# Two transformer blocks on one core: context products in 64x64 tiles, a sixth buffer for MLP weights, constants in one allocation

## The chip, the cores and the metric

The kernel runs on one core of a Trainium2 chip. Time is device time in microseconds of that core, and a kernel's time is the median of its runs. Everything is in fp32. The engines are named as in the profile: PE (TensorE, with PEld for its weight loads), DVE (VectorE), ACT (ScalarE), POOL (GpSimd) and SP (SyncE, which here issues all DMAs, in order).

## What is computed

The input `x` has 32 sequences of 64 tokens with 512 features. Two blocks follow one another. The first is attention with 8 query heads and one shared key and value head of size 64, rotary positions, and then a gated MLP of width 2048; both normalisations are RMS with a scale that depends on the sequence. The second is attention with 16 heads of size 32 over 4 key and value heads that come out of a latent of 128, with a layer norm whose scale and shift depend on the sequence. Cut to what matters:

```python
# block 0
h = ada_rms(x, t, ln1_w, ln1_tw)
q, k, v = h @ Wq.T, h @ Wk.T, h @ Wv.T            # 8 heads of 64; one k, one v
q, k = rope(q), rope(k)
attn = softmax(q @ k.T / sqrt(64))                # within a sequence of 64
x = x + (attn @ v) @ Wo.T
h = ada_rms(x, t, ln2_w, ln2_tw)
x = x + (silu(h @ Wg.T) * (h @ Wu.T)) @ Wd.T      # 512 -> 2048 -> 512
# block 1
h = ada_layernorm(x, t)
q = h @ Wq.T; c = h @ Wkd.T; k = c @ Wku.T; v = c @ Wvu.T
x = x + attention(rope(q), rope(k), v) @ Wo.T
```

## The kernel before

The 2048 tokens are cut into 8 units of 256 tokens (4 sequences). A unit lives in SBUF as `x[128, 4, 256]`: features on partitions, in four chunks, tokens in the free dimension. For each unit there are three pieces of work: `attention0` (block 0's attention and the norm of the MLP), `mlp`, and `attention1`.

**MLP.** Each of the three weight matrices is multiplied by seven products of halves (Strassen's scheme) instead of eight. One "set" is a buffer `[128, 7, 256]` with the three quarters of weights that are used as they are, and four sums of them. For the first unit, a set is loaded as three quarters (384 KB, `set<-in_wmlp`) and a fourth one (128 KB, `a<-in_wmlp`), `combine` makes the four sums on DVE and POOL, and they are stored to DRAM (512 KB, `sums<-set`). From the second unit on the sums are loaded back (`set<-sums`). Three sets (gate, up, down) serve one of eight pairs of hidden tiles; 192 sets in all pass through `MW` = 5 buffers with the tag `mw`. `load_sets` issues the next load when `done_with` says that a set is used up. `first_products` and `last_products` make the products `gu`, `gated` the activations, `down` the second matmul.

**attention0** is a generator that yields (cost, latency) after each piece. Queries `q0` and the pair of keys and values `kv0` are projected with weights stationary and tokens moving. Values are turned by transposes `vt` and copied by ACT into `vblk0`, which holds, for each sequence, a block-diagonal matrix of 128 x 128: the values in the upper left for the even heads and in the lower right for the odd heads, zeros elsewhere. These zeros are written once, by POOL (`early`). Probabilities `p` are transposed in two halves `t` (`turned`: four transposes into a bank `pp`, and a copy by ACT to `pT`), and for each half two matmuls of K=128, M=128, N=256 make the context `cx`, which two ACT copies per half of 128 x 256 bring to `cT`. `output` then multiplies `cT` with `wo0` in two halves, `po`, and adds to `x`.

**Order.** The instructions of the first two attentions are recorded in the order of the string `FIRST` ("a" is unit 0, "b" unit 1, "m" the modulations), and on PE this order is binding. They run before there is any MLP work. After that the class `Order` mixes the MLP of unit u, `attention0` of unit u+1, and `attention1` of earlier units, always the one that is least advanced among those whose latency is over. A scheduler of the framework then sorts each engine's queue further, and inserts the waits. PSUM has 8 banks: two with the tag `at` for all attention work beside the MLP, two `gu`, four `acc` for the `down` sums.

**At the end** the last two units' `attention1` run without MLP, with buffers borrowed from elsewhere (`sixth`, `seventh`); the seventh takes the first `vblk0`, zeroed again, for its values.

Constants and weights that stay (`ident`, `spread`, `small`, `kblk0`, `vblk0`, `wqkv`, `wo0` and so on) are each a tile of their own, made by `fixed`.

Of the kernel before, what the change touches and what calls it, by code (L numbers as in the profile page):

```python
# [10 lines left out]
F32 = mybir.dt.float32  # L11
# [6 lines left out]
P = 128  # L18
B, S, D = 32, 64, 512
# [25 lines left out]
TURN = (0.15911865234375, 3.628432750701904e-05, 6.4192136051133275e-09, 1.4247115856860781e-12)  # L45
ROUND = 12582912.0
WARM = 11
FIRST = "aaaaaaa bb a mm aa b a b aa bbb a b aa a bb a mmmm a bbbb".replace(" ", "")
TWO_PI = float(np.nextafter(np.float32(2 * np.pi), np.float32(0)))


# [56 lines left out]
def two_blocks(ctx: ExitStack, tc: tile.TileContext, a: dict, out: bass.AP):  # L108
# [17 lines left out]
        homes["n"] += 1  # L126
        return bank(tags[homes["n"] % len(tags)], name)

    def fixed(tag, shape, dtype=F32):
        return const.tile(shape, dtype, tag=tag, name=tag)  # L130

    def work(tag, shape, name, bufs=2):
        return wk.tile(shape, F32, tag=tag, name=name, bufs=bufs)


    ident = fixed("ident", [P, P])
    make_identity(nc, ident)
    ones = fixed("ones", [P, P])
    nc.gpsimd.memset(ones, 1.0 / D)

    idle = bank("at", "idle")
    for _ in range(WARM):
        nc.tensor.matmul(idle[:, :P], ones, ones, start=True, stop=True)

    spread = fixed("spread", [P, US, P])
    nc.gpsimd.memset(spread, 0.0)
    for q in range(US):
        rows = slice(q * HALF0, (q + 1) * HALF0)
        for i in range(2):
            block = ident[rows, rows][:, i * HALF1 : (i + 1) * HALF1].unsqueeze(1).unsqueeze(1)  # L150
            to = spread[rows, q].rearrange("p (r a h f) -> p r a h f", r=2, a=2, h=2)[:, :, i]
            nc.gpsimd.tensor_copy(to, block.to_broadcast([HALF0, 2, 2, HALF1]))
    eps0 = fixed("eps0", [P, 1])
    nc.gpsimd.memset(eps0, EPS0)
    eps1 = fixed("eps1", [P, 1])
    nc.gpsimd.memset(eps1, EPS1)
    quarter = fixed("quarter", [P, 1])
    nc.gpsimd.memset(quarter, float(np.float32(np.pi / 2)))

    positions = []  # L160
# [4 lines left out]
        positions.append(t)  # L165

    load_positions(0)
    small = fixed("small", [P, C_ALL])
    nc.sync.dma_start(small, a["small"])
    condT = small[:, C_COND:C_VECS].rearrange("p (k b) -> p k b", b=B)  # L170
    vecs = small[:, C_VECS:C_CS1]
# [3 lines left out]
    sign_of = small[:, C_SIGN:C_ALL]  # L175


    kblk0 = [fixed(f"kblk0{i}", [P, US, S]) for i in range(2)]

    vblk0 = [fixed(f"vblk0{i}", [P, US, 2, S]) for i in range(2)]  # L180
    vblk1 = [fixed(f"vblk1{i}", [P, US, 2, 2 * HD1]) for i in range(2)]

    s0a = fixed("s0a", [P, KC, B])
    s0b = fixed("s0b", [P, KC, B])
    s1 = fixed("s1", [P, KC, B])
    t1 = fixed("t1", [P, KC, B])
    angle = fixed("angle", [P, 2, NU * S])


    wqkv = [fixed("wqkv0", [P, KC, 384]), fixed("wqkv1", [P, KC, 256])]  # L190
    wo0 = fixed("wo0", [P, KC, D])
    wq1 = fixed("wq1", [P, KC, D])
    wkd = fixed("wkd", [P, KC, LAT])
    wkv1 = fixed("wkv1", [P, 2, P])
    wo1 = fixed("wo1", [P, KC, D])

    x_units = {}

# [4 lines left out]
        nc.sync.dma_start(xt, a["x"][u])  # L203
        x_units[u] = xt

    MW = 5

# [98 lines left out]
    def angles(u0):  # L308

        cols = slice(u0 * S, (u0 + 2) * S)  # L310

        def some(tag, name, cols=512, bufs=2):
            return work(tag, [P, cols], f"{name}_{u0}", bufs)[:, : 2 * S]

        posi = positions.pop()
        posf, sign = some("u", "posf"), some("v", "sign")
        both = work("p0", [P, 2, 512], f"ang_lo_{u0}", 1)
        ang, lo = both[:, 0, : 2 * S], both[:, 1, : 2 * S]
        hi, prod = some("pT0", "hi", 512, 1), some("r0", "prod", UT, 1)
        acc, rnd = angle[:, 0, cols], angle[:, 1, cols]  # L320
        nc.vector.tensor_copy(posf, posi)
        nc.vector.tensor_scalar(sign, posf, 0.0, None, ALU.is_ge)
        nc.vector.tensor_scalar(sign, sign, 2.0, -1.0, ALU.mult, ALU.add)
        nc.vector.tensor_tensor(posf, posf, sign, ALU.mult)
        nc.vector.tensor_scalar(ang, posf, freq, None, ALU.mult)
        nc.vector.scalar_tensor_tensor(lo, ang, 4097.0, ang, ALU.mult, ALU.subtract)
        nc.vector.scalar_tensor_tensor(hi, ang, 4097.0, lo, ALU.mult, ALU.subtract)
        nc.vector.tensor_tensor(lo, ang, hi, ALU.subtract)

        def fraction(dst, src):  # L330
            nc.vector.tensor_scalar(rnd, src, ROUND, ROUND, ALU.add, ALU.subtract)
            nc.vector.tensor_tensor(dst, src, rnd, ALU.subtract)

        first = True
        for piece, turn in ((hi, 0), (hi, 1), (lo, 0), (hi, 2), (lo, 1)):
            nc.vector.tensor_scalar(prod, piece, TURN[turn], None, ALU.mult)
            if first:
                fraction(acc, prod)
                first = False
            else:  # L340
                fraction(prod, prod)
                nc.vector.tensor_tensor(acc, acc, prod, ALU.add)
        nc.vector.scalar_tensor_tensor(acc, lo, TURN[2], acc, ALU.mult, ALU.add)
        nc.vector.scalar_tensor_tensor(acc, ang, TURN[3], acc, ALU.mult, ALU.add)
        fraction(prod, acc)
        nc.vector.tensor_scalar(lo, prod, 0.25, None, ALU.add)
        fraction(hi, lo)
        nc.scalar.activation(acc, hi, AF.Sin, scale=TWO_PI)
        nc.scalar.activation(rnd, prod, AF.Sin, scale=TWO_PI)
        nc.vector.tensor_tensor(rnd, rnd, sign, ALU.mult)  # L350
        if u0 + 2 < NU:
            load_positions(u0 + 2)
# [75 lines left out]
    def all_chunks(row):  # L428
        return row.unsqueeze(1).to_broadcast([P, KC, UT])

    RING = {"h": 2, "p1": 2, "pT1": 2}

    def space(room, tag, columns, name):

# [6 lines left out]
    def tile4(room, tag, name):  # L441
        return space(room, tag, KC * UT, name).rearrange("p (c t) -> p c t", t=UT)
# [126 lines left out]
    def attention0(u, room, early=None, late=None):  # L569
# [71 lines left out]
        vt = abank(f"vt_{u}").rearrange("p (b d) -> p b d", d=P)  # L641
        for b in range(US):
            nc.tensor.transpose(vt[:, b, :HD0], vT[HD0:, b].rearrange("p r s -> p (r s)"), ident[HD0:, HD0:])
        for i in range(2):
            rows = slice(i * S, (i + 1) * S)
            nc.scalar.copy(vb[rows, :, i, :], vt[rows, :, :HD0])
        yield 0.3, 4.5


# [23 lines left out]
            yield 0.5 * len(ts), 5.0 * ts[0] if lean else 10.0  # L673

        cT = tile4(room, "h", f"cT0_{u}")
        for t in range(2):
            pT = turned(ps[t], f"0_{u}_{t}", space(room, "pT", 512, f"pT0_{u}_{t}")).rearrange("p (c t) -> p c t", c=KC)
            yield 0.5, 1.2
            cx = abank(f"cx0_{u}_{t}").rearrange("p (b c s) -> p b c s", b=2, c=KC)
            for b in range(2):  # L680
                nc.tensor.matmul(  # L681
                    cx[:, b],
                    vb[:, 2 * t + b].rearrange("p r d -> p (r d)"),
                    pT[:, :, b * S : (b + 1) * S],
                    start=True,
                    stop=True,
                )
            to = cT[:, :, t * P : (t + 1) * P].rearrange("p c (b s) -> p b c s", s=S)
            for b in range(2):
                nc.scalar.copy(to[:, b], cx[:, b])  # L690
            yield 0.9, 1.5 * t
        yield from output(u, cT, wo0, f"0_{u}")


# [293 lines left out]
                load_sets(MW)  # L988

    def early():  # L990
        for z in (*vblk0, *vblk1):
            nc.gpsimd.memset(z, 0.0)

    def second(u, room=None):
# [61 lines left out]
    def spare(tag, cols, name, bufs=2):  # L1056
        return work(tag, [P, cols], f"own_{name}", bufs)

    nc.gpsimd.memset(vblk0[0], 0.0)
    two = [spare("h2", 1024, f"h2{i}") for i in range(2)]  # L1060
    few = spare("cs", 512, "few", 1)
    extra = spare("x", 1024, "kb6", XB)
# [5 lines left out]
        "latT": [few[:, :UT]],  # L1068
        "kr": [few[:, UT:]],
        "kb": [extra[:, :512]],  # L1070
        "pT": [extra[:, 512:], spare("pT0", 512, "pT6", 1)] * 2,
    }
    big = [spare("mw", 1792, f"mw{j}", MW) for j in range(4)]
    seventh = {
        "ring": "-",
        "lean": True,
        "vb": vblk0[0],
        "h": [big[0][:, :1024], big[1][:, :1024], big[1][:, :1024]],
        "latT": [big[0][:, 1024:1280]],
        "kr": [big[0][:, 1280:1536]],  # L1080
# [89 lines left out]
```

## Time and profile before

| what | value |
|---|---|
| median of 3 runs | 1061.24 us (1060.54 to 1062.72) |
| the profiled execution's own time | 1059.08 us |
| its span | 1057.3 us |
| mean granted PE clock | 0.989 |
| `gu` matmuls, two groups | 288.3 and 215.3 us busy |
| `down` matmuls, two groups | 136.4 and 109.2 us busy |
| `po`, largest group | 108.4 us busy, 480 instructions of 380 ns |
| context of attention 0 (`cx`, line 681) | 18.3 us busy, 64 instructions |
| bytes moved by DMA | 198.53 MB, mean 188 GB/s |

A row of a group gives its busy time, the mean duration of one instruction, and the idle time of the engine just before. Durations of PE instructions overlap, since they are pipelined, so what a block of them costs is read from the start of its first to the start of the next block in the timeline. A matmul of the program is two instructions of the same shape in the trace.

### The profile page before, as it was taken

To read this page: it belongs to the slowest core of one execution; us is meant where nothing else is said; L and a number is where in the kernel's file an instruction comes from. 1 tells how busy PE (TensorE), PEld (TensorE's weight loads), DVE (VectorE), ACT (ScalarE), POOL (GpSimd) and SP (SyncE) were. 2 spreads that over 40 slices of the span, in tenths; PEclk is the share of its full clock that TensorE was granted. 3 is DMA by queue.
4 is the path that set the end of the run, shared out by engine and by line. 5 is a ranking of instruction groups with operands and counts; after the bars stand their busy time and mean duration, and the time that the engine had idled before them with its cause. 6 is when DMAs were issued, how large, how long until landed. Compare 5 with 4: busy or idle time off the path is not lost.

```text
span 1057.3 us, 21448 instructions
## 1 busy us (share of the span) xinstructions
PE 1013.2 (96%) x8538; PEld 944.1 (89%) x8538; DVE 548.6 (52%) x1377; ACT 324.5 (31%) x682; POOL 434.7 (41%) x520
## 2 busy tenths in 40 slices
PE   7889999999999989999999998999999999999887
PEld 6779999998999989999999997999999899999765
DVE  4866646543455485343653268532755335452363
ACT  4333112344124242132422323331423422241132
POOL 4424545344255434254342543324533335432541
PEclk8989999999999999999999999999999999999899
DMA  7916896354556465662646555455735557565001
GB/s 276 328 43 219 294 312 240 136 210 151 203 210 210 143 217 177 227 222 105 224 172 221 184 182 183 150 203 203 251 118 196 173 189 284 197 230 178 11 1 40
DMA packets 68274, 198.53 MB, mean 188 GB/s; under 512 B 7248, under 2 KB 15184, under 8 KB 67792
## 3 DMA queue, kind: packets, MB, share of 16 engines
q1 hardware_dynamic: 68176, 197.17, 53.6%
q8 instruction: 68, 1.11, 0.4%
q14 instruction: 30, 0.25, 0.1%
HBM read 180.37 MB, written 16.78 MB: 186 GB/s over the span
## 4 chain that ended last, share of the span: by engine, by line
PE 79%; DVE 10%; POOL 5%; issue 2%; DMA 2%; ACT 1%; SPq 0%; ACTq 0%; POOLq 0%; DVEq 0%
PE gu L875 32%; PE down L934 16%; PE po L514 10%; PE q L514 9%; PE pp L549 2%; PE lat L514 1%; PE cx L681 1%; PE cx L845 1%; PE sc L821 1%; PE kv L514 1%; DMA set<-in_wmlp 1%; PE sc L664 1%; DVE mx L534 1%; DVE sm L542 1%; DMA x<-in_x 1%
## 5 line engine op out<-in xcount | busy, mean ns | idle before, releaser
L875 PE MATMUL gu<-h,set 128*128 128x128 f32 x2048 | 288.3, 276 | 8.9 <-DVE c L894 5.2
L875 PEld LDWEIGHTS gu<-h,set 128*128 128x128 f32 x2048 | 259.4, 192 | 15.9 <-issue 10.7
L875 PE MATMUL gu<-hc,set 128*128 128x128 f32 x1536 | 215.3, 275 | 0.0
L875 PEld LDWEIGHTS gu<-hc,set 128*128 128x128 f32 x1536 | 193.6, 192 | 0.5
L913 POOL TENSOR_TENSOR act<-c,c 128x384 f32<-128x384 f32 x64 | 66.6, 1040 | 193.6 <-DVE c L901 117.5
L934 PE MATMUL down<-td,set 128*128 128x128 f32 x1024 | 136.4, 276 | 3.2 <-POOL td L916 3.2
L934 PEld LDWEIGHTS down<-td,set 128*128 128x128 f32 x1024 | 125.1, 192 | 4.5 <-POOL td L916 4.2
L887 ACT COPY e<-gu 128x128 f32<-128x128 f32 x128 | 33.7, 265 | 279.1 <-PE gu L875 268.8
L901 DVE TENSOR_TENSOR c<-gu,u 128x256 f32<-128x256 f32 x128 | 53.4, 419 | 118.1 <-PE gu L875 117.8
L514 PE MATMUL po<-cT,wo 128*128 128x256 f32 x480 | 108.4, 380 | 2.4 <-DVE sm L542 2.1
L934 PE MATMUL down<-act,set 128*128 128x128 f32 x768 | 109.2, 278 | 0.0
L889 DVE TENSOR_TENSOR u<-e,gu 128x128 f32<-128x128 f32 x128 | 36.1, 282 | 130.4 <-ACT e L887 129.8
L514 PEld LDWEIGHTS po<-cT,wo 128*128 128x128 f32 x480 | 89.3, 190 | 14.2 <-ACT cT L854 2.6
L934 PEld LDWEIGHTS down<-act,set 128*128 128x128 f32 x768 | 97.9, 192 | 4.2 <-issue 2.4
L544 POOL TENSOR_TENSOR p<-p,sm 128x512 f32<-128x512 f32 x40 | 41.3, 1052 | 116.5 <-DVE sm L543 110.6
L525 POOL TENSOR_TENSOR qT<-u_q,v_q 128x512 f32<-128x512 f32 x30 | 38.1, 1270 | 93.8 <-DVE v_q L524 93.8
L562 DVE TENSOR_TENSOR x<-x,po 128x512 f32<-128x512 f32 x32 | 22.0, 687 | 75.9 <-PE po L514 75.9
L970 ACT ACT_TABLE_LOAD x34 | 43.6, 1283 | 55.8 <-DVE c L901 55.4
L514 PE MATMUL q<-h,wqkv 128*128 128x256 f32 x256 | 58.4, 380 | 0.0
L514 PE MATMUL q<-h,wq 128*128 128x256 f32 x224 | 52.1, 385 | 1.6 <-POOL h L750 1.6
L514 PEld LDWEIGHTS q<-h,wqkv 128*128 128x128 f32 x256 | 47.7, 191 | 6.4 <-issue 0.4
L915 POOL TENSOR_TENSOR td<-act 128x256 f32<-128x256 f32 x64 | 47.6, 744 | 10.0 <-DVE act L912 3.8
(276 smaller groups left out, 1407.4 us busy)
## 6 DMA issues: line engine op xcount, KB each, us to landing
set<-sums SPq DMA_DIRECT2D x168, 512.0 KB, 5.8
set<-in_wmlp SPq DMA_DIRECT2D x192, 384.0 KB, 4.7
sums<-set SPq DMA_DIRECT2D x24, 512.0 KB, 4.7
x<-in_x SPq DMA_DIRECT2D x8, 512.0 KB, 5.7
out_x<-x SPq DMA_DIRECT2D x16, 256.0 KB, 2.1
mod<-in_mod SPq DMA_DIRECT2D x7, 512.0 KB, 6.2
a<-in_wmlp SPq DMA_DIRECT2D x24, 128.0 KB, 4.3
wo<-in_wo SPq DMA_DIRECT2D x2, 1024.0 KB, 8.4
```

What stands on the lines that cost most here:

```text
L514: nc.tensor.matmul(ps, w[:, k, cols], h[:, k, :], start=(k == 0), stop=(k == KC - 1))
L525: nc.gpsimd.tensor_tensor(dst, u, v, ALU.add)
L544: nc.gpsimd.tensor_tensor(p8, p8, sm.unsqueeze(2).to_broadcast(wide), ALU.mult)
L562: nc.vector.tensor_tensor(x[:, part], x[:, part], po, ALU.add)
L875: nc.tensor.matmul(ps, w[:, slot, k * P : (k + 1) * P], b[of][:, k], start=start and k == 0, stop=k == 1, skip_group_check=True)
L887: nc.scalar.copy(e, ps[:, 0])
L889: nc.vector.tensor_tensor(u2, e, ps[:, 1], ALU.add)
L901: nc.vector.tensor_tensor(c.rearrange("p (a b) t -> p a b t", b=2)[:, :, 1], ps[:, 2:4], u2.unsqueeze(1).to_broadcast([P, 2, HT]), ALU.add,)
L913: nc.gpsimd.tensor_tensor(act[:, 1:4], gate[:, 1:4], c[:, 1:4], ALU.mult)
L915: nc.gpsimd.tensor_tensor(td[:, 0:2], act[:, 1:3], act[:, 0:2], ALU.subtract)
L934: nc.tensor.matmul(sums_of[u][p][:, c], w[:, slot, c * P : (c + 1) * P], b[of], start=q % NP == 0 and i % 2 == 0 and c == 0, stop=q % NP = ...
L970: nc.scalar.activation(gate[2][:, 0], gate[0][:, 0], AF.Silu)
```

## The change

- **Context of attention 0.** `vblk0` is no longer block-diagonal but `[128, 4, 64]`: the values of a sequence twice, above one another, filled by one ACT copy of 128 x 256 in place of two of 64 x 256. For each half `t`, each sequence `b` and each half of the rows `r` there is one matmul with K=64, M=64, N=256, so eight in place of four. The tiles lie at the four corners of the array: rows by `r`, columns by `b`. Results go to two banks, one per `r`. Both halves of `p` are transposed first, and `cT` is filled at the end by four ACT copies of 64 partitions x 512.
- **Order.** `attention0` has one yield fewer, other costs and latencies, and `FIRST` has one "a" less. The "bbbb" at its end now reaches into unit 1's first half of `po`.
- **Sets.** `MW` is 6.
- **One buffer.** `fixed` cuts its tiles out of a single one of 14103 columns, `stays`.
- **Small.** The angle computation takes three buffers of its own (`ang0` to `ang2`) in place of `p0` and `pT0`; `pT0` has two buffers; the zeros of `vblk0` and their memsets go; at the end the seventh's values get a zeroed buffer with the tag `pT1`.

The projections of queries and of outputs (`query`, `project`, `output`) are not touched by the diff.

```diff
-FIRST = "aaaaaaa bb a mm aa b a b aa bbb a b aa a bb a mmmm a bbbb".replace(" ", "")
+STAY = 14103
+FIRST = "aaaaaaa bb a mm aa b a b a bbb a b aa a bb a mmmm a bbbb".replace(" ", "")
...
+    stays = {"all": const.tile([P, STAY], F32, tag="stays", name="stays"), "at": 0}
+
+    def fixed(shape):
+        n, i = int(np.prod(shape[1:])), stays["at"]
+        stays["at"] += n
+        t = stays["all"][:, i : i + n]
...
-    vblk0 = [fixed(f"vblk0{i}", [P, US, 2, S]) for i in range(2)]
+    vblk0 = [fixed([P, US, HD0]) for i in range(2)]
...
-    MW = 5
+    MW = 6
...
-        both = work("p0", [P, 2, 512], f"ang_lo_{u0}", 1)
-        ang, lo = both[:, 0, : 2 * S], both[:, 1, : 2 * S]
-        hi, prod = some("pT0", "hi", 512, 1), some("r0", "prod", UT, 1)
+        ang, lo, hi = (some(f"ang{i}", f"ang{i}", 2 * S, 1) for i in range(3))
+        prod = some("r0", "prod", UT, 1)
...
-    RING = {"h": 2, "p1": 2, "pT1": 2}
+    RING = {"h": 2, "p1": 2, "pT0": 2, "pT1": 2}
...
-        for i in range(2):
-            rows = slice(i * S, (i + 1) * S)
-            nc.scalar.copy(vb[rows, :, i, :], vt[rows, :, :HD0])
+        nc.scalar.copy(vb, vt[:, :, :HD0])
         yield 0.3, 4.5
...
         cT = tile4(room, "h", f"cT0_{u}")
+        pTs = []
         for t in range(2):
-            pT = turned(ps[t], f"0_{u}_{t}", space(room, "pT", 512, f"pT0_{u}_{t}")).rearrange("p (c t) -> p c t", c=KC)
-            yield 0.5, 1.2
-            cx = abank(f"cx0_{u}_{t}").rearrange("p (b c s) -> p b c s", b=2, c=KC)
+            pT = turned(ps[t], f"0_{u}_{t}", space(room, "pT", 512, f"pT0_{u}_{t}"))
+            pTs.append(pT.rearrange("p (c t) -> p c t", c=KC))
+            yield 0.5, 1.2 * t
+
+        banks = [abank(f"cx0_{u}_{r}").rearrange("p (t c s) -> p t c s", t=2, c=KC) for r in range(2)]
+        for t in range(2):
             for b in range(2):
-                nc.tensor.matmul(
-                    cx[:, b],
-                    vb[:, 2 * t + b].rearrange("p r d -> p (r d)"),
-                    pT[:, :, b * S : (b + 1) * S],
-                    start=True,
-                    stop=True,
-                )
-            to = cT[:, :, t * P : (t + 1) * P].rearrange("p c (b s) -> p b c s", s=S)
+                for r, cx in enumerate(banks):
+                    rows = slice(r * S, (r + 1) * S)
+                    nc.tensor.matmul(
+                        cx[b * HD0 : (b + 1) * HD0, t],
+                        vb[rows, 2 * t + b],
+                        pTs[t][rows, :, b * S : (b + 1) * S],
+                        start=True,
+                        stop=True,
+                    )
+        by_two = cT.rearrange("p c (t b s) -> p t c b s", b=2, s=S)
+        for r, cx in enumerate(banks):
             for b in range(2):
-                nc.scalar.copy(to[:, b], cx[:, b])
-            yield 0.9, 1.5 * t
+                nc.scalar.copy(by_two[r * HD0 : (r + 1) * HD0, :, :, b], cx[b * HD0 : (b + 1) * HD0])
+        yield 1.1, 2.5
         yield from output(u, cT, wo0, f"0_{u}")
...
     def early():
-        for z in (*vblk0, *vblk1):
+        for z in vblk1:
             nc.gpsimd.memset(z, 0.0)
...
-    nc.gpsimd.memset(vblk0[0], 0.0)
+    zeros = spare("pT1", 512, "vb7", 2).rearrange("p (b r d) -> p b r d", b=US, r=2)
+    nc.gpsimd.memset(zeros, 0.0)
...
-        "vb": vblk0[0],
+        "vb": zeros,
```

## The prediction

> **What bounds the kernel now.** I read the busy shares and the chain of waits first. Matmuls are busy 96% of the span and the chain runs through PE for 79% of it, so in most stages only fewer PE passes, or less PE waiting, can shorten anything.
>
> ```profile
> PE 1013.2 (96%) x8538; PEld 944.1 (89%) x8538; DVE 548.6 (52%) x1377; ACT 324.5 (31%) x682; POOL 434.7 (41%) x520
> ...
> PE 79%; DVE 10%; POOL 5%; issue 2%; DMA 2%; ACT 1%; SPq 0%; ACTq 0%; POOLq 0%; DVEq 0%
> ```
>
> PE is idle for 44 us of 1057.3. The table of stretches (length, then busy us and instructions of PE, PEld, DVE, ACT, POOL, then granted clock, DMA share, GB/s) says where.
>
> ```profile
> 20.00:40.00 20.00, 16.62 (x207) 13.96 (x206) 16.80 (x39) 5.70 (x11) 10.40 (x13) 1.00 0.71 226
> 40.00:60.00 20.00, 16.81 (x202) 14.21 (x200) 15.90 (x37) 8.27 (x16) 6.84 (x7) 1.00 0.80 321
> 60.00:80.00 20.00, 18.18 (x120) 15.99 (x121) 13.50 (x48) 5.99 (x12) 3.96 (x4) 0.74 0.01 2
> ...
> 100.00:120.00 20.00, 19.41 (x176) 19.25 (x172) 14.30 (x40) 4.04 (x10) 9.88 (x14) 1.00 0.85 278
> 120.00:140.00 20.00, 18.96 (x170) 18.80 (x169) 11.47 (x36) 2.45 (x8) 10.32 (x14) 1.00 0.95 316
> ...
> 300.00:500.00 200.00, 196.06 (x1631) 185.02 (x1632) 102.93 (x261) 60.84 (x131) 88.05 (x98) 1.00 0.54 187
> ```
>
> From such rows, PE idle is 13.9 us in the first 80 us (two attentions with no MLP beside them), 1.6 us in 80 to 160 (the first unit's MLP, when its sets are built and stored), 14.4 us in 160 to 985, and 13.8 us in the tail. The tail's order on PE is the same in both programs, so I leave it at 0. The change touches the other three.
>
> **The announced seven products for queries and outputs are not in the code.** Comparing the programs' PE orders, the changed one has 4415 matmuls, the old one 4383; the 32 more are the context products of attention 0 (four per unit become eight). Had `q` and `po` lost an eighth in six units, their 19% of the chain (202 us) would have given 202 × 6/8 × 1/8 = 19 us. I give that no chance.
>
> **Part 1, context in 64x64 tiles (-1.4 us in 160 to 985).** Each matmul is two passes in the trace. The timeline shows the old product and the nearest row to the new one: scores of attention 1, also 64x64 tiles over two row halves and two column halves.
>
> ```profile
> 223.43 1.03 PE L681 MATMUL cx<-pT,vblk 128*128 128x256 f32 x4
> 224.29 0.60 PE L549 MATMUL pp<-ident,p 128*128 128x128 f32 x4
> 224.73 0.61 PE L875 MATMUL gu<-h,set 128*128 128x128 f32 x4
> ...
> 238.83 1.08 PE L845 MATMUL cx<-pT,vblk 128*64 128x256 f32 x8
> 239.84 0.71 PE L875 MATMUL gu<-h,set 128*128 128x128 f32 x4
> ...
> 243.61 1.10 PE L821 MATMUL sc<-kb,qT 64*64 64x128 f32 x32
> 244.65 0.60 PE L875 MATMUL gu<-h,set 128*128 128x128 f32 x3
> ```
>
> Start to start, four old passes take 0.86 us, so a unit pays 1.73. The score block streams 32 × 128 = 4096 columns in 1.04 us; one after another at 0.216 us per 256 columns they would take 3.46, so four tiles run at once, with 0.18 us on top. The new product is 16 × 256 = 4096 columns: again 1.04. Now a rule against the change: the Trainium skill, "TensorEngine Tiling (Array Packing)", Tiling Modes, says that switching the tiling mode drains the array. The row prices it: PE comes 0.09 us late into the score block (previous work should end at 243.52), and the first `gu` after a tiled block spends 0.10 us more (0.71 against 0.61). So a block costs 1.23 and a unit gains 0.50; the bare four-fold reading would say 0.86. The program's order spoils two units: in unit 2 the tiles stand so that they pack into three rounds instead of two (1.67, gain 0.06), and in unit 4 the two row halves are split by other work, so each runs two at a time like L845 and pays the switch twice (2.40, loss 0.67). Units 3, 5, 6, 7 gain 4 × 0.50; together 1.4 us. Ends: all four-way and no switch 5.2, a gain of nothing 0.
>
> **Part 2, the later, longer copies (+0.8 us there).** ACT's groups at 31 to 48 us:
>
> ```profile
> L690 ACT COPY cT<-cx 128x256 f32<-128x256 f32 x4 | 1.3, 376 | 1.7 <-PE cx L681 1.7
> L550 ACT COPY pT<-pp 128x512 f32<-128x512 f32 x2 | 1.2, 594 | 3.5 <-PE pp L549 3.5
> ```
>
> Four copies of 256 columns (two after each half) become four of 512, all after the last product: 4 × 0.594, or about 2.1 us where they overlap by 0.1 each. `po` needs all of them. The value copy falls from two of 0.364 to one of about 0.376. The same page's PSUM Bottleneck section warns that evacuation becomes the limit once matmuls are packed; the row agrees in kind. In the order, 2.7 to 5.2 us of other PE work stand between product and `po` in the middle units, so 2.1 us is covered unless ACT is behind a SiLU (table load 1.28, then 0.28 and 0.52). I take 0.2 us in four units. Ends: 0, and 0.8 in six units, 4.8. Behind the copies on ACT stand `e` and the SiLU, for which `gu` waits; that is in the same bound. Both `at` banks are now held at once; the scheduler put work on other banks there.
>
> **Part 3, the first 80 us (-0.3 us).** Three things move. (a) On DVE the third combine now stands ahead of the first score maximum: three operations of about 0.42 us, while DVE had 0.34 idle there: +0.8 before the softmax. SP issues that set at about 20.5 and its `a` at 27.5, in an idle DMA stretch, so data is not late; `wo0` slips from 20.5 behind that wait to 27.9 and, at its 8.4 us, lands by 36.3 (needed after 47). The modulations slip about 2 us, needed at 57. (b) Unit 0's first context product no longer sits between the transposes (-0.9), the whole block comes later (1.04 for 0.88), and `po` waits for 2.1 us of copies where it waited 0.6:
>
> ```profile
> 46.66 0.66 ACT cT L690 x2
> 47.32 0.04 issue
> 47.36 7.19 PE po L514 x32
> ```
>
> That puts `po` at about 48.9, +1.5. (c) From 62 to 72 us the clock was granted at 0.50, and there unit 1's context took 2.07 + 1.50 us, with a 0.68 us wait between. The new block takes about 2.0 there and its two transposes run together. Walking PE forward from `row_b` (66.2 instead of 64.7), by 76.8 us four more `gu` passes are done and 0.7 fewer of `po`: 0.3 us ahead. Ends: +1.5 (nothing won back) and -4 (the half-clock stretch ends early). The memsets removed from POOL stood before an `h` that waited 6.0 us for `s0a`: 0. The three new angle tiles change no operation, only buffers: 0. That weights start at odd 4-byte offsets in the single buffer no row shows; passes of 0.216 us cover their loads (0.19), so 0, at worst a little on the first loads.
>
> **Part 4, the sixth set (-1.6 us in 80 to 160).** Each hidden pair needs three sets of 1.05 MB (two loads, one store) in 9.4 us: 334 GB/s, while DMA at share 0.95 moves 316. It is just short, and twice the chain goes through a late set:
>
> ```profile
> 101.81 5.21 DMA set<-in_wmlp
> ...
> 124.85 5.45 DMA set<-in_wmlp
> ```
>
> PE idles 0.59 and 1.04 us behind those. A sixth buffer lets one more set, 3.1 us of work, be fetched before 80, when DMA is at share 0.01. Both waits should go; next late is DVE's own queue. Ends: 0 and 1.6. No PE wait after 160 ends with a set's DMA, so nothing more there.
>
> **Sum.** -1.4 + 0.8 - 0.3 - 1.6 = -2.5 us. The profiled execution took 1059.08 us, 1.8 more than its span and 2.2 below the median 1061.24; applied to the median: **1058.7 us**. About 0.2%, 2.1 us, is what can be told from no change.
>
> **Rivals.**
> 1. *The copies eat it.* `po` waits 0.8 us in each of six middle units: +4.8 for +0.8, 1062.7; with half of that 1060.7, inside 0.2%. For it: ACT holds a 2.1 us block in one piece, before `po` and in front of SiLU. Against: the order keeps 2.7 us or more between. Chance 0.33 for staying within 0.2%.
> 2. *Slower: the clock drops once more.* Place: before the first transposes. PE waited 2.16 us there at full clock; with 3(a) it waits 2.9 to 3.0. After the 2.73 us wait at 58 to 60.7 the clock fell to 0.50 for 10 us. The Trainium skill, "TensorE: Matmul & The Clock Gate", section on why this matters, warns of idle gaps over about 3 us. By the row, 2.7 us before light work can be enough, by the rule 2.9 just escapes; I go with the rule, since here dense `q` passes stand right before. If it falls, about 10 us of half clock over dense work costs 5 us: 1063.7. It decides once that wait exceeds about 3 us. With worse copies also here, chance 0.15.
> 3. *More:* half clock ends earlier, and no copy is late: -0.8 - 3 us more, 1054.9. It lies in the chance of faster, 0.52.
>
> The range runs from 1054.0 (rival 3 and a little) to 1063.4 (rivals 1 and almost 2).
>
> **What would show it.** Context blocks of about 1.04 us, 1.7 to 2.4 in units 2 and 4; no chain step through a set's DMA between 100 and 135; `po` of unit 0 at about 49; a half-clock stretch that still ends near 72; few `po` waits on `cT`. Wrong, if half clock appears near 40, if `po` waits on ACT by 0.5 us or more per unit, or if 300 to 900 shows more PE idle than before.

## The result, and the profile after

The changed kernel takes 1058.27 us, the median of 20 runs (1055.39 to 1063.30), beside 1062.78 us for the kernel before in 20 runs on the same chips (1059.06 to 1064.93). The ratio is 0.9964, 95% interval 0.9950 to 0.9979: by the ratio 3.8 us faster (2.2 to 5.3). The same kernel was measured once more among the experiments: 0.9970 (0.9957 to 0.9983). The forecast was 1058.7 us and 2.5 us gained.

The profiled execution of the changed kernel is a long one, 1062.67 us (span 1060.9, mean granted clock 0.982), and that of the kernel before, 1059.08 us, was among its shortest. So the two pages laid side by side show a *loss* of 3.6 us. A second profile of the changed kernel (run `after2` below) has a span of 1057.2 us. I use both, and say which.

From the page of the changed kernel (first profile), busy shares and the chain of waits:

```profile
PE 1015.9 (96%) x8602; PEld 940.9 (89%) x8602; DVE 544.6 (51%) x1377; ACT 329.8 (31%) x674; POOL 431.6 (41%) x518
...
PE 81%; DVE 10%; POOL 4%; ACT 2%; DMA 1%; issue 1%; SPq 0%; ACTq 0%; DVEq 0%; POOLq 0%
```

The bound is what it was. PE has 64 passes more, which are the 32 more context products; the queries' and outputs' products are as many as before. The table of stretches, for the rows shown of before (columns as there):

```profile
20.00:40.00 20.00, 16.06 (x198) 13.29 (x196) 16.27 (x40) 4.75 (x9) 10.29 (x13) 1.00 0.61 203
40.00:60.00 20.00, 16.85 (x204) 14.27 (x208) 14.99 (x34) 7.11 (x14) 7.41 (x7) 1.00 1.02 387
60.00:80.00 20.00, 16.73 (x135) 13.57 (x128) 15.16 (x48) 9.57 (x13) 5.08 (x5) 0.74 0.04 12
...
100.00:120.00 20.00, 18.84 (x167) 18.52 (x167) 13.16 (x39) 2.44 (x8) 10.39 (x14) 1.00 0.85 277
120.00:140.00 20.00, 20.00 (x182) 20.00 (x181) 12.36 (x37) 2.44 (x8) 10.38 (x14) 1.00 0.92 320
140.00:160.00 20.00, 19.35 (x174) 19.19 (x173) 9.45 (x31) 2.70 (x9) 8.24 (x12) 1.00 0.91 311
```

Between 80 and 160 us PE is still idle: 1.16 us in 100 to 120 and 0.65 in 140 to 160, together 1.82 with the 0.01 of 80 to 100 (1.63 before). The sixth set has not taken the two waits away. (Such a figure is one of a single execution: `warmp`, `warmt` and `warmpt` below have the same order on SP's queue and show 1.93, 2.21 and 0.52 us.) The chain of the same profile goes through a late set twice, as before:

```profile
105.41 5.08 DMA set<-in_wmlp
...
135.14 5.95 DMA set<-in_wmlp
```

**The steady part is exact, and it gained 1.04 us.** ACT copies the first of a unit's down sums once per unit, and these eight copies are good marks. From that of unit 0 to that of unit 7 it takes 823.63 us before and 822.59 after. Five kernels with the new context and six sets (`after2`, `a3`, `pst`, `warmp` and `warmt` below) repeat each of the seven stretches within 0.03 us. The table of stretches for the units from 1 on, before:

```profile
158.74:284.36 125.62, 123.10 (x1020) 115.61 (x1019) 60.80 (x146) 42.37 (x84) 53.08 (x60) 1.00 0.55 193
284.36:406.23 121.87, 118.57 (x1004) 111.50 (x1003) 70.56 (x181) 39.66 (x83) 53.37 (x60) 1.00 0.55 187
...
646.97:762.70 115.73, 113.14 (x964) 106.41 (x965) 58.31 (x138) 37.35 (x73) 48.58 (x57) 1.00 0.56 195
762.70:885.67 122.97, 122.97 (x1018) 115.38 (x1017) 57.76 (x143) 38.54 (x79) 44.69 (x54) 1.00 0.53 184
```

and after (second profile, which has no half clock there):

```profile
158.40:283.43 125.03, 122.97 (x1028) 115.02 (x1027) 60.11 (x146) 42.63 (x82) 52.04 (x60) 1.00 0.56 194
283.43:406.01 122.58, 118.46 (x1012) 110.90 (x1011) 70.11 (x181) 40.27 (x83) 53.26 (x60) 1.00 0.55 186
...
646.61:760.58 113.97, 113.03 (x977) 106.17 (x976) 55.53 (x136) 38.27 (x72) 47.70 (x55) 1.00 0.59 199
760.58:884.44 123.86, 123.65 (x1026) 115.07 (x1025) 58.12 (x148) 40.49 (x79) 48.63 (x58) 1.00 0.53 181
```

The first number is the length of the stretch. For the seven it changes by -0.59, +0.71, +0.65, -0.79, -1.76, +0.89 and -0.15 us. The gain is not a fixed sum per unit. In the first three of the four stretches shown it goes with PE's idle time (length less busy time: -0.46, +0.82 and -1.65 us); in the fourth PE is busy 0.68 us longer. The sums over the seven stretches, for the kernel before, for `after2`, and for `mw5a4` below, which has the new context and five sets:

```profile
sum 823.63, PE 809.19 PEld 763.14 DVE 408.41 ACT 257.32 POOL 339.17; mean PE 115.60 PEld 109.02 DVE 58.34 ACT 36.76 POOL 48.45
sum 822.59, PE 809.05 PEld 759.61 DVE 404.31 ACT 261.04 POOL 337.68; mean PE 115.58 PEld 108.52 DVE 57.76 ACT 37.29 POOL 48.24
sum 821.58, PE 808.00 PEld 758.93 DVE 404.45 ACT 261.73 POOL 337.74; mean PE 115.43 PEld 108.42 DVE 57.78 ACT 37.39 POOL 48.25
```

PE's busy time is almost what it was (-0.14 us); the gain is idle time (14.44 to 13.54 us). And the sixth set is no part of it: with five sets the same stretches are 1.01 us shorter still (`mw5` repeats six of the seven within 0.03 us; the other has a piece of half clock). So the context with its order gains 2.05 us here, and the sixth set takes 1.01 back, in busy time; why, the runs do not show.

So about 1 us of the 3.2 to 3.8 is settled here. The rest must be ahead of unit 0's mark (the first 160 us), in the tail, or in the clock. The experiments are about that.

### The profile page after: what moved, and what is told of

Read it like the earlier page. It is cut to its first block, busy times and chain, and to the rows that moved or that the text cites. A ratio compares the mean times of both kernels' runs of the same rounds, so it can differ in the third digit from the quotient of the medians.

```text
span 1060.9 us, 21476 instructions
## 1 busy us (share of the span) xinstructions
PE 1015.9 (96%) x8602; PEld 940.9 (89%) x8602; DVE 544.6 (51%) x1377; ACT 329.8 (31%) x674; POOL 431.6 (41%) x518
## 4 chain that ended last, share of the span: by engine, by line
PE 81%; DVE 10%; POOL 4%; ACT 2%; DMA 1%; issue 1%; SPq 0%; ACTq 0%; DVEq 0%; POOLq 0%
PE gu L891 33%; PE down L950 16%; PE po L525 10%; PE q L525 9%; PE pp L560 2%; PE cx L861 2%; PE sc L837 1%; PE lat L525 1%; PE kv L525 1%; DMA set<-in_wmlp 1%; DVE mx L545 1%; PE sc L673 1%; PE cx L696 1%; DVE sm L553 1%; PE tab L400 1%
## 5 line engine op out<-in xcount | busy, mean ns | idle before, releaser
L525 PE MATMUL po<-cT,stays 128*128 128x256 f32 x480 | 109.3, 384 | 4.4 <-DVE sm L553 2.3
L525 PE MATMUL q<-h,stays 128*128 128x256 f32 x480 | 110.5, 383 | 1.7 <-POOL h L766 1.2
L525 PEld LDWEIGHTS po<-cT,stays 128*128 128x128 f32 x480 | 90.7, 193 | 17.4 <-ACT cT L870 2.7
L525 PEld LDWEIGHTS q<-h,stays 128*128 128x128 f32 x480 | 90.2, 192 | 14.2 <-POOL h L766 1.4
L986 ACT ACTIVATE c<-gu 128x128 f32<-128x128 f32 x64 | 17.7, 277 | 97.7 <-DVE c L917 89.4
```

The costliest lines, as they stand in the source:

```text
L525: nc.tensor.matmul(ps, w[:, k, cols], h[:, k, :], start=(k == 0), stop=(k == KC - 1))
L986: nc.scalar.activation(gate[2][:, 0], gate[0][:, 0], AF.Silu)
```

## The experiments

All kernels are the changed one with an edit. One thing was not visible in the source: memory is packed from the tiles' lifetimes, so the number of buffers asked for is not the number of places a tile goes round. In the compiled programs `a21` (asked: 2) goes round four places before, three after, and two with five sets. A load of `a21` (`a<-in_wmlp` in the profile) into a place that is still being read waits for DVE's combine, on SP's in-order queue. The summary, with PE idle in 80 to 160 us from the one profile of each:

| kernel | context, sets | `a21` places | of 24 `a21` loads, wait for DVE | ratio (95%) | PE idle, us |
|---|---|---|---|---|---|
| before | old, 5 | 4 | 1 | 1 | 1.63 |
| changed | new, 6 | 3 | 10 | 0.9964 (0.9950-0.9979) | 1.82 |
| `after2` | same | same | 10 | 0.9970 (0.9957-0.9983) | 2.66 |
| `oldcx5` | old, 5 | 2 | 20 | 1.0019 (1.0009-1.0029) | 3.49 |
| `oldcx6` | old, 6 | 3 | 7 | 1.0001 (0.9991-1.0011) | 2.10 |
| `mw5` | new, 5 | 2 | 20 | 1.0006 (0.9993-1.0018) | 4.33 |
| `mw5a4` | new, 5 | 4 | 10 | 0.9985 (0.9975-0.9995) | 3.49 |
| `a3` | new, 6 | 3 | 19 | 1.0044 (1.0027-1.0060) | 7.54 |
| `a4` | new, 6 | 4 | 17 | 0.9978 (0.9967-0.9989) | 4.17 |
| `pst` | new, 6 | 3 | 19 | 1.0068 (1.0044-1.0091) | 5.09 |
| `split` | new, 6 | 3 | 11 | 1.0012 (1.0001-1.0023) | 5.57 |

### Undoing the sixth set, the context, or both

`mw5`:

```diff
-    MW = 6
+    MW = 5
```

> The changed kernel with five MLP sets in place of six; all else as changed. Theory of the prediction (the sixth set takes both waits behind sets out, 1.6 us): the ratio to before rises from 0.9964 to about 0.998, and PE waits 1.5 us or more longer between 100 and 145 us than with six sets. Rival (the trace of the changed kernel still shows 1.16 and 0.65 us of PE idle behind two sets, so the sixth set brings nothing): the ratio stays at 0.9964 within 0.001, and the idle behind sets is again 1.6 to 2.0 us.

1.0006: the whole gain is gone, 3.8 to 4.5 us by the ratios, more than twice what the prediction gave the set. PE idles 4.33 us in 80 to 160. Neither theory had it so large, and "brings nothing", which the trace of the changed kernel alone suggested, is wrong.

`oldcx5` and `oldcx6`: the old context (whole tiles of 128x128, block-diagonal `vblk0`, old order list), with five and with six sets.

```diff
-        banks = [abank(f"cx0_{u}_{r}")... for r in range(2)]
+        for t in range(2):
...
+            cx = abank(f"cx0_{u}_{t}").rearrange("p (b c s) -> p b c s", b=2, c=KC)
...
-STAY = 14103
+STAY = 14615
```

> The changed kernel with the old block-diagonal context (four products of 128x128 tiles per unit, old order list) and five sets: of the change only the single buffer, the separate angle tiles and the second pT0 are left. Both theories: ratio 1.000 within 0.001. If odd starts in the single buffer cost weight loads, it is above 1.001, and PEld's mean grows.

> The changed kernel with the old block-diagonal context, but six sets. If the sixth set is worth 1.6 us as predicted: 0.9985. If the context alone makes the gain: 1.000 within 0.001. If the two only work together (the sixth set moves the start, the context uses it): 1.000 here and 1.000 with five sets and the new context.

`oldcx5` is 1.0019: 2.0 us *slower* than before, with nothing left of the change but the single buffer, three angle tiles, a second `pT0` and a tile of zeros used in the tail. Slow weight loads would show in every unit, and its units 2 to 6 take 121.91, 115.42, 125.38, 115.75 and 122.98 us, within 0.07 of before. What differs is ahead of unit 0's mark, where PE idles 3.49 us: `a21` has two places left, and 20 loads wait. Both theories missed it, because both had read the new layout as costing nothing. With six sets and the old context (1.0001) a third of the changed kernel's advantage over `oldcx5` comes back. By the ratios the set is worth 1.9 us with the old context and 3.8 to 4.5 with the new one, the context 1.4 us with five sets and 3.3 to 3.9 with six, each within about 1.5 to 2 us. This is what the third theory of `oldcx6` had put on record, that the two only work together: 1.0001 and 1.0006 where it said 1.000 and 1.000. But the extra worth of having both, 1.9 to 2.6 us by these ratios, is itself known only within about 2.5 us, and the places of `a21` change along with the sets.

### Places for `a21`, or its place in the queue?

`a3` and `a4` ask for three and four buffers, `mw5a4` for four with five sets:

```diff
-                odd[n] = work("a21", [P, 2 * P], f"a21_{n}", 2)
+                odd[n] = work("a21", [P, 2 * P], f"a21_{n}", 4)
```

> The changed kernel with three buffers in place of two for a21, the quarter of a hidden pair's set that is combined on DVE. Theory (set loads stand on the sync queue behind a21 loads that wait for the combine, so six sets cannot be fetched ahead): the idle of PE behind sets between 100 and 145 us falls from 1.8 to below 0.5 us, ratio about 0.995. Rival (DMA is full there, share 0.85 to 0.95, so order of issue does not matter): idle stays 1.5 us or more, ratio 0.9964 within 0.001.

1.0044, 8 us slower than the changed kernel: the largest surprise. The compiled `a3` uses the same three places in the same turn as the changed kernel, and PE's order is the same (on DVE some combines stand a place or two elsewhere). What differs most is SP's queue: the scheduler, told of a third buffer, puts the `a21` loads from 46 us on a place or two earlier there, so that in the same place of the queue stands the load for a later set. The timeline of the sync queue (start, time until issued), changed kernel:

```profile
93.76 3.90 SPq L242 DMA_DIRECT2D set<-in_wmlp  x3
97.70 0.43 SPq L245 DMA_DIRECT2D a<-in_wmlp  x1
101.37 0.33 SPq L263 DMA_DIRECT2D sums<-set  x1
```

and `a3`:

```profile
93.39 3.90 SPq L242 DMA_DIRECT2D set<-in_wmlp  x3
100.95 0.33 SPq L245 DMA_DIRECT2D a<-in_wmlp  x1
101.38 0.38 SPq L263 DMA_DIRECT2D sums<-set  x1
```

In the changed kernel `a` goes out 0.04 us after the sets; in `a3` the queue stands for 3.7 us until DVE has combined, then `a` is late. Twenty microseconds on, a load waits from 118.6 to 122.4 in the same way, the next sets go out at 127.5 in place of 124.4, and PE pays (rows of the stretches of `a3`; the second column is PE's busy time of 20):

```profile
100.00:120.00 20.00, 18.65 (x163) 18.16 (x162) 11.28 (x35) 2.44 (x8) 10.37 (x14) 1.00 0.76 255
120.00:140.00 20.00, 16.42 (x141) 15.77 (x141) 11.71 (x35) 2.17 (x7) 8.07 (x10) 1.00 0.77 261
140.00:160.00 20.00, 17.40 (x156) 17.24 (x155) 8.76 (x30) 1.75 (x6) 8.94 (x12) 1.00 0.89 287
```

DMA's share (the number before the last) is lower than in the changed kernel, 0.76 and 0.77 for 0.85 and 0.92: in `a3` the DMA engines were not short of bandwidth, they were not given work. So an order of the queue can cost up to 8 us (how much of it is DVE's changed order was not taken apart). The rival "DMA is full there" is answered for `a3` alone; for the two waits of the changed kernel, at shares of 0.85 to 0.92, it stays open.

> The changed kernel with five sets and with four buffers for a21 (the old kernel's a21 went round four places, the changed one's round three, and with five sets round two). Theory A (what five sets lost against the old kernel, 2.7 us more PE idle in 80 to 160 us, is the lost a21 places, not the set): idle in 80 to 160 falls from 4.3 to about 1.6 us and the ratio from 1.0006 to about 0.998. Theory B (the sixth set is worth it by itself, a21 does not matter): stays at 1.0006 within 0.001.

0.9985: theory A on the ratio (from 1.0006, 2.2 us for the two places, known within about 1.7), but the idle fell only to 3.49 us, not to 1.6. Against before, `mw5a4` has the old number of sets and of places and the new context and layout; it gains 1.6 us (0.5 to 2.7).

> The changed kernel (six sets) with four buffers for a21. With three declared, the time went to 1.0044 although the loads used the same three places in the same turn: the scheduler put each a21 load one or two places earlier on the sync queue, where it waits for DVE's combine and holds up the stores and set loads behind it. Theory A (place on the queue decides): a4's loads stand early too and wait for DVE, so the ratio is above 1.000 and PE idles more than 4 us in 80 to 160. Theory B (number of places decides): idle below 1.8 us, ratio at or under 0.9964.

0.9978: neither. The idle, 4.17 us, is theory A's, but the ratio is below 1.000. Four places are better than `a3`'s three, but 17 loads wait; against the changed kernel the ratio is 0.8 to 1.5 us worse, which the intervals do not tell from nothing. What orders the table is roughly the number of loads that stand on SP's queue waiting for DVE, not the places: 1 to 10 loads for 0.5 to 3.5 us of idle, 17 to 20 for 3.5 to 7.5. It is an ordering, not a law: `split` has 11 and 5.57 us, and five traces with one and the same queue (the changed kernel twice, and the three with added matmuls below) range from 0.52 to 2.66.

`pst` takes the stores off SP's queue:

```diff
-            nc.sync.dma_start(kept[3 * (q % NP) + m], sets[n][:, 0:4])
+            nc.gpsimd.dma_start(kept[3 * (q % NP) + m], sets[n][:, 0:4])
```

> The changed kernel with the stores of the sums issued from GpSimd, right behind the combine's last operation there, and no longer from the sync queue, so that no set load or a21 load stands behind a store. Theory A (the sync queue's order keeps the two waits behind sets): PE idle in 80 to 160 falls from 1.8 to under 0.6 us, ratio about 0.995. Theory B (DMA is full there): idle stays at 1.5 us or more. Cost to be seen beside it: GpSimd's own time for issuing 24 stores, which may delay its combines and make it worse than 0.9964.

1.0068, the slowest. It did not test what it was meant to: without the stores in front of them, whose own wait for POOL had covered the combine, 19 `a21` loads instead of 10 now wait for DVE. And POOL spends 0.57 to 0.72 us on issuing each store, in front of the next combine:

```profile
104.63 0.78 POOL L258 TENSOR_TENSOR set<-set 128x256 f32<-128x256 f32 x1
105.71 0.57 POOL L263 DMA_DIRECT2D sums<-set  x1 [0.30 <-DVE c L910]
106.81 0.72 POOL L258 TENSOR_TENSOR set<-set 128x256 f32<-128x256 f32 x1 [0.53 <-DVE set L256]
```

So that a queue without such waits would clear the idle entirely was not shown.

### The later copies

```diff
-                nc.scalar.copy(by_two[...], cx[...])
+                e = nc.vector.tensor_copy if lean and r else nc.scalar.copy
+                e(by_two[...], cx[...])
```

> The changed kernel with the copies of one half of the context (two of four, in units 0 and 1) on DVE in place of ACT. The prediction's step 3b says that po of unit 0 waits for four copies one after another on ACT: it should start 1.0 to 1.2 us earlier (at about 48.9 in place of 50.0), ratio 0.995. Rival (the first 80 us are set by DVE, 10% of the chain, and DVE takes the copies at the cost of the softmax of unit 1): po earlier, but first gu no earlier, ratio 0.9964 or more.

1.0012, 4.5 to 5 us worse, and `po` did not start earlier (50.67 us). The two copies on DVE wait there behind the rotation of unit 1 and end at 50.4, in DVE's timeline of `split`:

```profile
48.27 0.72 DVE L535 STREAM_SHUFFLE v_q<-v_q 128x512 f32<-128x512 f32 x1
49.02 1.39 DVE L707 COPY cT<-cx 64x512 f32<-64x512 f32 x2
```

So 2.1 us of copies on ACT are the cheaper place. But the loss itself does not lie there. In the profile of `split`, which like `after2` has no half clock near 70 us, the first `gu` comes at 69.15 us for 68.59; from it to unit 0's mark it takes 95.10 us for 89.81, with 5.57 us of PE idle between 80 and 160 and a DMA share of 0.75 in 100 to 120 for 0.94. The loss is in the supply of sets again; SP's queue has another order in a few places, and whether that is the cause was not tried. The rival had the right side of 0.9964, but not the place, and `po` was not earlier as it said.

### The clock

> The changed kernel itself, unchanged, once more. Ratio 0.9964 within 0.0015. If the half-clock stretches fall by chance of time and not by program, its trace has other ones than the first trace of it (which had 10.2 us at the start, 10.2 at 62 to 73, 3.4 at 254, 6.8 at 990 and twice 3.4 in the tail).

The half-clock stretches did change. In the first profile 10.2 us of half clock lay at 63 to 73; in the second there are none, and PE gets its first `gu` at 68.59 in place of 71.86. The tail has the same ones in both. Every stretch of half clock (granted clock 0.50) in these 14 traces, save those that the end cuts off, is a multiple of 3.41 us (3.4, 6.8, 10.2, 13.7). The Trainium skill, "TensorE: Matmul & The Clock Gate", Part 1, says why: activity is judged in windows of 3413 ns that run free and do not restart with the kernel. The traces agree. They also show what the clock goes by. Cut by each trace's own grid, there are 4187 windows at full clock after the first 17 us. All 28 in which PE was busy for less than 0.41 of the window are followed by half clock; of the 82 between 0.41 and 0.58, 22 are; of the 4077 above, 5, all of them at 987 to 998 us. So what counts is not the length of a wait but how much of it falls into one window. The wait of 2.96 us before unit 0's first transposes lies for the most part in one window in `warmp` (an experiment below, without an edit up to there), and half clock (0.50) follows:

```profile
36.75:40.16 3.41, 1.39 (x7) 0.88 (x5) 3.41 (x12) 0.98 (x2) 0.29 (x1) 1.00 0.94 284
40.16:43.58 3.42, 2.48 (x12) 2.48 (x13) 3.21 (x3) 0.59 (x1) 3.01 (x4) 0.50 0.99 287
```

In the first profile of the changed kernel the same wait is cut in half between two windows, and the clock stays:

```profile
35.38:38.79 3.41, 1.91 (x9) 1.33 (x7) 3.41 (x10) 1.26 (x2) 0.00 (x0) 1.00 0.97 308
38.79:42.21 3.42, 1.97 (x18) 1.97 (x19) 3.42 (x6) 0.91 (x3) 3.19 (x3) 1.00 0.96 270
```

In the same way, where the grid lies at the end of unit 7 decides the tail. The last three rows of stretches of `after2`, the number before the DMA share being the granted clock:

```profile
985.00:1010.00 25.00, 21.98 (x155) 18.87 (x156) 10.89 (x22) 7.97 (x18) 12.69 (x11) 0.86 0.00 1
1010.00:1030.00 20.00, 15.88 (x187) 11.47 (x185) 15.22 (x33) 7.88 (x21) 8.29 (x8) 0.91 0.01 2
1030.00:1061.00 31.00, 21.30 (x96) 16.32 (x96) 7.67 (x16) 5.37 (x12) 4.13 (x4) 0.89 0.09 35
```

and of `a4`, with the same tail, product for product on PE:

```profile
985.00:1010.00 25.00, 21.70 (x167) 18.50 (x166) 12.10 (x26) 7.98 (x18) 14.76 (x14) 1.00 0.00 1
1010.00:1030.00 20.00, 15.50 (x187) 11.38 (x185) 16.12 (x35) 8.53 (x22) 8.28 (x8) 0.91 0.01 2
```

| a window begins, us after unit 7's mark | half clock in the tail, without the last 4 us | tail, us |
|---|---|---|
| 0.61 to 1.26 (`oldcx6`, `mw5a4`, before, `oldcx5`) | 6.8 | 74.4 to 75.1 |
| 2.30 to 2.44 (`a3`, `split`, `a4`) | 3.4 + 3.4 | 73.1 to 73.2 |
| 2.75 to 3.40 (`pst`, changed, `mw5`, `after2`, `warmp`) | 6.8 + 3.4 + 3.4 | 76.0 to 76.5 |

So 3.4 us of one profile are chance of phase, about as large as the whole effect of the change. That is why the two first profiles could not be compared by their spans. Of the 3.6 us by which that of the changed kernel is longer, 1.86 lie ahead of unit 0's mark, 1.16 in the tail, and 0.58 between, where one window of half clock at 254 us costs 1.6.

Can the clock be held up? `warmp` puts matmuls of ones into the wait at 60.6 us before the third modulation's transpose, `warmt` into four waits of the tail, `warmpt` both:

```diff
+    def warm(to, n):
+        for _ in range(n):
+            nc.tensor.matmul(to, ones, ones, start=True, stop=True)
...
+        warm(pt[:, :P], (0, 0, 12, 0)[i])
         nc.tensor.transpose(pt[:, :P], rows, ident)
```

> The changed kernel with 12 matmuls of ones (128x128, result overwritten) put into the 2.83 us wait before the transpose of the third modulation at 60.6 us; the order on every other queue is the same. The half-clock stretch at 62 to 73 should be gone, and the first gu be at about 67 in place of 71.9. Theory A (the end of the first unit's MLP is set by the stream of sets through DMA): PE idle in 80 to 160 grows by most of what is won, and the ratio falls by 0.001 or less, to about 0.9955. Theory B (half clock there costs its full 5 us, as my prediction's rivals 2 and 3 had it): ratio about 0.992.

> The changed kernel with matmuls of ones in four waits of the tail (4 before the second qs_c, 6 before the lat of unit 6, 9 before its first transposes, 9 before its po), order on every other queue the same. If half clock in the tail costs time: no stretch of it after 985, the tail from the last unit's end (76.1 us in the first trace) at or under 73.5, ratio about 0.9945. Rival (the tail waits for DVE and POOL, PE's clock does not matter there, and the added matmuls delay what comes): 0.9964 or more.

> Both of the two before. If they add up: the sum of the two gains, about 0.9935 by theory A for the first; a version that would beat both kernels.

`warmp`: 0.9952 (0.9932 to 0.9972), the ratio that theory A named, but not to be told apart from the changed kernel (0.9964, 0.9970), with a median of 1059.12 us in 11 runs beside 1059.65, and not by theory A's way: in its profile the first `gu` comes at 73.93 us, not at 67, and PE's idle in 80 to 160 is 1.93, not more. Half clock is gone at 63 to 73 and lies at 40 to 47 and 54 to 57 instead (0.74 in the first row), the second of them on the dense `po`:

```profile
40.00:60.00 20.00, 16.84 (x82) 14.30 (x83) 13.10 (x27) 5.38 (x11) 6.34 (x6) 0.74 1.03 392
60.00:80.00 20.00, 18.11 (x265) 15.35 (x264) 15.38 (x46) 11.20 (x15) 7.01 (x6) 1.00 0.07 24
```

The added matmuls did not move it there, for they come later, at 65.9 us; it is the phase of the grid. Whether they keep half clock away at 63 to 73 one trace cannot say. `warmt` is a clear miss: 1.0004 (0.9989 to 1.0018). Two stretches of half clock, of 6.8 us each, are still in its tail, and the tail takes 81.2 us for 76.1. `warmpt` (0.9996, 0.9979 to 1.0013) has a single window in its tail and still takes 76.9 us. So the tail's time is not the clock alone; that the added matmuls stand in the way of what follows is likely, but ACT's and DVE's order also differs from the changed kernel's in a few places there, and neither was tried further. No version here is shown to beat the changed kernel.

**How much of the gain is clock?** Every run's mean granted clock is recorded. Over the three groups of experiments the kernel before was granted 0.9837 to 0.9847 on average (161 runs); the changed kernel 0.9882 and 0.9869 (42 runs). At or below 0.984 there are too few runs to tell: in the last group 1064.5 us (median of 40 of 56 runs of before) beside 1064.4 (4 of 22 of `after2`) and 1063.0 (4 of 20 of the first measurement). Within the runs of one kernel the span rises by 0.52 to 0.72 us (by the group of runs) for each us of (1 - clock) times the span. By that fit `after2` is 0.5 to 1.2 us shorter than before at equal clock, and the first measurement of the changed kernel 1.4 to 2.7; another 1.8 to 3.5 us come with the clock. Of the traces, those with the old context have 10.2, 6.8 and 10.2 us of half clock at 62 to 73; eight with the new context (none with added matmuls) have 10.2, 0, 10.2, 3.4, 6.8, 0, 6.8 and 0, though three of these have 3.4 us more that begin between 41 and 53. It fits with the block of products and both transposes now standing together there, without the 0.68 us wait between them. It is a count of 11 traces, not an experiment: which windows the mean clock is won in stays open.

## Why the prediction came out right, point by point

The time was right, 1058.7 beside 1058.27 us, and that closeness is partly luck: the forecast started from a median of 1061.24 us, and the kernel before took 1062.78 beside the changed one. The gain of 2.5 us was short by about 1 (3.8 and 3.2 by the two ratios), and it came by other ways than the sum had: the layout, put at nothing, measured +2.0; the sixth set did not do what it was to do and costs 1.0 in the steady part; the new context gains more there than forecast; and a part comes with the clock.

- **Part 1, size and price of the blocks: right.** Predicted 1.23 us per unit with 0.09 before and 0.10 behind. The timeline of `after2` at unit 6:

```profile
708.53 0.61 PE L891 MATMUL gu<-h,set 128*128 128x128 f32 x4
709.07 1.09 PE L696 MATMUL cx<-pT,stays 64*64 64x256 f32 x16
710.10 0.71 PE L950 MATMUL down<-act,set 128*128 128x128 f32 x4
710.64 1.50 PE L950 MATMUL down<-td,set 128*128 128x128 f32 x12
```

  Start to start the block is 1.03; the four passes before take 0.54 and those behind 0.54, for 0.445 undisturbed: 1.22 in all. Units 5, 6 and 7 are so. Start to start and without the ends, unit 3's block takes 1.18, unit 2's 1.33 where 1.48 was predicted; unit 4's two halves take 1.02 + 1.01, with two pairs of switches 2.43 for 2.40. The skill's rule that a change of tiling mode drains the array ("TensorEngine Tiling (Array Packing)", Tiling Modes) agrees with the 0.095 us at each end; a drain itself no row shows.
- **What Part 1 left out: the neighbours.** Added up start to start over 160 to 985, the blocks fell from 11.02 to 7.62 us, but `gu` rose by 1.7, `down` by 0.9, attention 1's context by 0.6 and `var` by 0.4. Seven blocks with a switch at both ends explain 1.3 of these 3.6; attention 1's tiled context is now cut by other work in one more place; the rest I could not place. So the passes won on the blocks were paid out again, and the net gain is PE's idle (-0.90 us), which Part 1 did not name. The sum of -1.04 stands beside -1.4 + 0.8 predicted, and it is -2.05 for the context with five sets and +1.01 for the sixth set, of which Part 4 said "nothing more there".
- **Part 2, the copies: a small cost, as forecast, but another one.** In the middle units PE waits for these copies twice: 0.12 us before `po` in unit 2, and once more in the waits of `after2`:

```profile
PE q L525 <- ACT cT L706: 0.6, 1, 0.6
```

  Together 0.67 us where 0.8 was taken. But the product that waits 0.56 us is a `q`, which does not read `cT`; most likely it wants one of the two `at` banks, which now stay held until the copies end. Part 2 named that and put no cost to it. Rival 1 (0.8 in each of six units) did not occur. (The section that Part 2 cites, PSUM Bottleneck of the skill's "TensorEngine Tiling (Array Packing)", says only that the copy out of PSUM may become the bottleneck.)
- **Part 3, the first 80 us.** (a) held: the wait before the first transposes is 2.96 us with the third combine ahead of the softmax (2.16 before; `oldcx5` to `oldcx6` moves it from 2.06 to 2.96 by the sixth set alone). (b) `po` of unit 0 starts at 50.01 where 48.9 was forecast; about 1 us of it is a later start of everything (0.9 at the first transposes beyond (a)), and its wait for the copies is 2.06 us as priced:

```profile
40.24 0.65 PE L560 MATMUL pp<-stays,p 128*128 128x128 f32 x4 [2.96 <-POOL p L555]
...
50.01 7.17 PE L525 MATMUL po<-cT,stays 128*128 128x256 f32 x32 [2.06 <-ACT cT L706]
```

  (c) "still ends near 72" is true of the first profile (73) and false of the second (no half clock there). It was a statement about one draw.
- **Part 4, the step that failed: "Both waits should go".** They stayed, in both profiles (1.82 and 2.66 us of idle for 1.63). The set's worth came out near all the same: `mw5a4` to the changed kernel is 1.6 to 2.2 us for 1.6 predicted, though each is known only within about 1.8, and the mechanism was not the one forecast. The other half of the failed step stood in Part 3 as "only buffers: 0": the new layout with five sets left `a21` two places for four, and `oldcx5` measured that layout at +2.0 us. By `oldcx6` (1.0001) the set about pays for this rise. I had read the sets' supply as a question of bytes per microsecond (334 GB/s against 316). The trace of `a3` shows DMA at 0.76 with PE starved, so there the order of one in-order queue came first; what holds the two waits in the changed kernel itself stays open.
- **Rival 2** (half clock near 40) is real but not as put: not a wait of 3 us decides. With the wait at 2.95 or 2.96 us, half clock began at 39.5 to 41.6 us in three traces (`warmp`, `warmt`, `warmpt`, all without an edit up to there) and not in six; in `mw5` it began at 40.9 after a wait of 2.07 us that lies whole in one window. So "2.9 just escapes" was luck of the grid in both profiles of the changed kernel. The page's warning of gaps over about 3 us is not the point at which it decides here. **Rival 3** (half clock ends earlier) was filed under "more" at 3 us for the whole; on average something of that size, 1.8 to 3.5 us, comes with the clock, in which windows is open.

## What to carry to other kernels

Before costing "the same buffers, elsewhere" at nothing, look at how many places each rotating tile really has and at which loads on an in-order queue wait for a compute engine: a buffer more can be worse, if the scheduler uses it to put a load ahead of others that could have gone. Where a kernel's effect is a few us, compare stretches between fixed marks (here the eight down sums, good to 0.05 us) and the mean clock of many runs, not the spans of two profiles. And in a stage fed by DMA, where a lower DMA share stands beside a more idle PE (0.76 for 0.85 in `a3`), look at the issuing queue before the bandwidth.

## What the runs showed of the hardware that I had not expected

The same tail takes 73.1 or 76.5 us by the phase of a grid of 3.41 us windows. In these traces a window with PE busy below 0.41 of it was followed by half clock every time (28 of 28), and a wait of 2.07 us could bring it where one of 2.96 did not. Single windows of half clock also stand in the middle, where the work is dense (at 252 to 258 us in five traces, at 389, 401 and 615 in others), each behind a window with PE busy 0.26 to 0.49 of it, and cost 1.2 to 1.6 us each. Matmuls of ones in a wait did not buy a faster tail: with 28 of them it took 81.2 and 76.9 us in two traces. And eight small products in 64x64 tiles pack as the scores do, four at once, to within 0.02 us, provided that they stand together.
